# Turning the mixed channels for their statistics: VectorE block transposes in place of TensorE transposes, in the last pass over the second image

## The chip, the cores and the metric

The kernel runs on one core of a Trainium2 chip. Its metric is the device time of one execution in microseconds (us), the median of several runs. Everything is computed in fp32.

## The reference, cut to what matters

Two layers work on `x` of shape (2, 56, 56, 384): two images of 3136 tokens with 384 channels. The first is a neighbourhood attention with an MLP behind it. The second, in which the change lies, is this:

```python
h = _layernorm(x, n1_g, n1_b)
p = h @ w_in + b_in                       # 384 -> 768 channels
local = depthwise_conv3x3(p, k_conv)
lr, rl = ema along W, both directions
tb, bt = ema along H, both directions
mixed = 0.25 * (lr + rl + tb + bt) + local
mixed = _layernorm(mixed, on_g, on_b)     # over the 768 channels of a token
x = x + (mixed @ w_out + b_out)           # 768 -> 384
h2 = _layernorm(x, n2_g, n2_b)
m = gelu(h2 @ w1 + b1) @ w2 + b2          # 384 -> 1536 -> 384
return x + m
```

The line that matters is the layer norm of `mixed`. It needs the mean and the variance of each token over its 768 channels.

## The kernel before, in words

The kernel has three parts: the attention (to about 710 us), a pass that runs the first layer's MLP and the second layer's `w_in` while VectorE computes the convolution and the scans beside it, and the last pass, which runs `w_out` and the second layer's MLP and writes the output.

The convolution and the scans work with channels on partitions, so the mixed channels lie in memory as `mix_d`, 6 blocks of 128 channels by 3136 tokens per image. The last pass walks over all 6272 tokens in 13 groups (`dgroups`): eleven of 4 tiles of 128 tokens, then one of 3 and one of 2. Image 1 begins in the middle of group 6, and this group is called `half_way`.

For each group `load_mix` loads `mx`, 128 partitions by 6 blocks by up to 512 tokens, again with channels on partitions, and the residual `x`. That layout is what `project_out` wants as the stationary operand of its matmul, but it isn't what the statistics want: `bn_stats` on VectorE reduces along the free dimension, so tokens have to be on partitions. Thus `measure` turns each tile of `mx` for this purpose alone. In it TensorE transposes 6 blocks of 128 x 128 into two PSUM tiles `xi` (from the pool `ps_t`, three buffers), and VectorE takes `bn_stats` of each half and `bn_aggr` of both. The normalization itself is folded into `w_out` and its rows; of the statistics only the reciprocal standard deviation (`rs`) is used later. It scales the result of `project_out` when VectorE evicts it from PSUM (line 1258).

The instructions of each engine are issued in the order of the program text. One iteration of the last pass for group g is:

- the hidden layer: twelve blocks m of 128 hidden channels, each of three fp32 matmuls (line 1035) followed by a GELU on ScalarE (line 1044). Beside it `measure_beside` measures group g+1, one tile every other block: at m = 3, 5, 7 and 9. At m = 10 `close` computes `rs`, an addition on VectorE (line 219) and a power on GpSimd (line 222);
- `project_out` of group g+1: for each tile 6 matmuls with `w_out` (line 1051), the eviction with `rs` by VectorE into `x3` (line 1258), and the statistics of `x3` for the next layer norm;
- the loads of group g+2;
- the output layer: for each tile 12 matmuls with `w2` (line 1051), an addition by VectorE (line 1432) and the store. Between its tiles lie ScalarE's normalization of `x3`, GpSimd's addition of a bias (line 987), and TensorE's transposes of the normalized `x3` (line 251).

Both `project_out` and the output layer write the PSUM tile `y` of the pool `ps_y`, which has two buffers. The SBUF pool `cp` has a tag `work` with two buffers, which the convolution and the scans use. They are finished before group 6 is loaded, because the loop calls `beside.until((1, NI - 1))` there.

Of the kernel before, what the change touches and what calls it, by code (L numbers as in the profile page):

```python
# [40 lines left out]
B, H, W, C = 2, 56, 56, 384  # L41
NH, KS, HD = 12, 7, 32
P = 128
NC = C // P
INNER, NI = 2 * C, 2 * C // P
# [128 lines left out]
def block_kernel(ctx: ExitStack, tc: tile.TileContext, ins: dict, out: bass.AP):  # L174
    nc = tc.nc
# [438 lines left out]
    def norm_of(x, n, small):  # L614
        norm = Norm(small)
        for k in range(n):
            norm.add(k, [x[:, k, :]])
        return norm
# [14 lines left out]
    for h in range(0, NT, 2):  # L633
        norm = Norm(sm)
# [51 lines left out]
    units, ws, to_project, ahead, taking = {}, {}, [], [], []  # L686
# [4 lines left out]
    for s in range(NU + 4):  # L691
        n, k, hg, i = s // UG, s % UG, s % NC, s // NC
# [100 lines left out]
    norm = norm_of(xs[0], groups[0][1], sm)  # L793
# [154 lines left out]
    def passes(xs, xn, w1, w2, between=lambda psum: None):  # L948
# [11 lines left out]
        half_way = next(g for g, (t, n) in enumerate(dgroups) if t + n * P > T1)  # L960
# [102 lines left out]
        def flat(t):  # L1063
            return t.rearrange("p a b -> p (a b)")

        def half(name, tag, bufs=2):
            return cp.tile([P, HALF, W], F32, name=name, tag=tag, bufs=bufs)
# [152 lines left out]
        def load_mix(g):  # L1220
            t0, n = dgroups[g]
            mx = io.tile([P, NI, MT], F32, name="mx")
            for b, at, here, n in images(t0, n * P):
                nc.sync.dma_start(
                    out=mx[:, :, here : here + n],
                    in_=mix_d[b][:, :, at : at + n].rearrange("m p t -> p m t"),
                )
            x = load_group(x2_d, dgroups[g], "xa")
            if g >= half_way:
                add_row(x, dgroups[g][1], "b_out")  # L1230
            return mx, x, Norm(sm)

        def measure(mx, norm, k):
            parts = []
            for h in range(2):
                ps = ps_t.tile([P, NC, P], F32, name="xi", tag="pt")
                for c in range(NC):
                    nc.tensor.transpose(  # L1238
                        ps[:, c, :], mx[:, h * NC + c, k * P : (k + 1) * P], ident
                    )  # L1240
                parts.append(ps.rearrange("p c q -> p (c q)"))
            norm.add(k, parts)

        def measure_beside(m, g, ahead):

            n = dgroups[g][1]
            if m % 2 == 1 and 0 < m // 2 <= n:
                measure(ahead[0], ahead[2], m // 2 - 1)
            if m == 10:
                ahead[2].close(n)  # L1250

        def project_out(g, mx, x, inner):
            n = dgroups[g][1]
            x3 = io.tile([P, NT, C], F32, name="xc")
            norm = Norm(sm)
            for k in range(n):
                ps = tokens([mx[:, c, :] for c in range(NI)], w_out, k)
                nc.vector.scalar_tensor_tensor(  # L1258
                    x3[:, k, :], ps, inner.rs[:, k : k + 1], x[:, k, :], ALU.mult, ALU.add
                )  # L1260
                norm.add(k, [x3[:, k, :]])
                beside.go(OUT_D)
            norm.close(n)
            return x3, norm
# [62 lines left out]
        for g, (t0, n) in enumerate(groups):  # L1327
            hid = []
            preparing = prepare_w_out() if g == 1 else iter(())
            if g == last:  # L1330
                beside.until((0, NI - 1))
                load_row(0, "b2_1")
                ahead = load_mix(0)
            for m in range(NHID):
# [27 lines left out]
                if g == last:  # L1362
                    measure_beside(m, 0, ahead)
# [14 lines left out]
            norm = Norm(sm)  # L1378
# [15 lines left out]
        g, x2, norm_w = waiting  # L1394
# [3 lines left out]
        x3, norm = project_out(0, *ahead)  # L1398
# [8 lines left out]
        ahead = load_mix(1)  # L1407
# [5 lines left out]
        for g, (t0, n) in enumerate(dgroups):  # L1413
            hid = []
            for m in range(NHID):
                hid.append(hidden(w1, m, hT, n, "L1_conv_b1"))
                if g < last:
                    measure_beside(m, g + 1, ahead)
                beside.go(MLP_D)
            res = x3  # L1420
            if g < last:
                x3, norm = project_out(g + 1, *ahead)
            if g + 2 <= last and g + 2 != half_way:
                ahead = load_mix(g + 2)
            for k in range(n):
                if k == n - 1 and g < last:
                    hT = channels(xn, dgroups[g + 1][1], "L1_conv_n2_g", "L1_conv_n2_b")
                ps = tokens(hid, w2, k)
                o = res[:, k, :]
                if k == 0 and g < last:  # L1430
                    norm.shift(dgroups[g + 1][1])
                nc.vector.tensor_tensor(o, ps, o, ALU.add)  # L1432
                nc.sync.dma_start(out=yout[t0 + k * P : t0 + (k + 1) * P, :], in_=o)
                if k == n - 3 and g < last:
                    xn = normalized(norm, x3, dgroups[g + 1][1])
                    add_row(x3, dgroups[g + 1][1], "b2_1")
                beside.go(ROW_D)
            if g + 2 == half_way:
                beside.until((1, NI - 1))
                ahead = load_mix(g + 2)  # L1440
        pctx.close()

    def raise_flag(psum):
        ps = psum.tile([P, C], F32, name="y")
        nc.tensor.matmul(ps[:1, :1], lhsT=bad, rhs=ones[:, :1], start=True, stop=True)
        nc.vector.tensor_scalar(flag, ps[:1, :1], 1.0, 0.0, ALU.min, ALU.add)

    passes(xs, xn, w1, w2, raise_flag)
    again = nc.values_load(flag[0:1, 0:1], min_val=0, max_val=1)
    with tc.If(again > 0):  # L1450
        attention_again()
        w1, w2, w_parts = weights(0)
        for part in w_parts:
            part()
        xs = {g: load_group(x1f, groups[g], "xa") for g in range(2)}
        with tc.tile_pool(name="small_again", bufs=1) as sm_again:
            norm = norm_of(xs[0], groups[0][1], sm_again)
            norm.close(groups[0][1])
            norm.shift(groups[0][1])
            xn = normalized(norm, xs[0], groups[0][1])  # L1460
        passes(xs, xn, w1, w2)
# [69 lines left out]
```

## Time and profile before

| what | value |
|---|---|
| time, median of 3 runs | 2735.04 us (2734.52 to 2737.29) |
| span of the profiled run | 2733.8 us |
| hidden layer of group 6, with the measuring of group 7 | 2237.5 to 2270.6, 33.1 us |
| `project_out` of group 7 | 2270.6 to 2286.1, 15.5 us |
| VectorE busy in these two stages | 5.46 us and 4.08 us |
| transposes `xi` from 2240 us on | 126, in 2247.0 to 2651.4 us |
| `bn_stats` on `xi` from 2240 us on | 42, 556 ns each |

In the profile a line names its engine (PE is TensorE's matmul, PEld its loading of weights, DVE VectorE, ACT ScalarE, POOL GpSimd), the line of the kernel, the operation, its output and input tiles with their shapes, and how often it ran. A matmul in fp32 shows as two records, and a transpose as one: line 1051 has 2352 records for `w2` where the program has 2 layers x 49 tiles x 12 matmuls = 1176. Matmuls are pipelined, so the length of a record is more than what it adds to the time; the distance from one start to the next is what it adds.

### The profile page before, as it was taken

The page shows a single profiled execution, that of the slowest core. Times are in us where ns is not written, and L with a number is a line of the kernel's source. Part 1 is how long each engine was busy: PE and PEld are TensorE (multiplying, and loading weights), DVE is VectorE, ACT ScalarE, POOL GpSimd, SP SyncE. Part 2 cuts the span into 40 slices and gives each one's busy share as a digit, 9 for nine tenths or more (in the row PEclk, how much of TensorE's full clock was granted, in tenths as well). Part 3 has the DMA queues.
Part 4 walks back from the last instruction along what each step waited for, and adds up shares of the span by engine and source line. Part 5 has one row for each costly group of instructions (what it writes and reads, how often), then busy time and mean ns, then how long its engine had stood idle before and what let it go on. Part 6 is the DMA issues. An engine that isn't in the chain of part 4 may idle for free. (4 is left out here: it accounts for less than half of the span.)

```text
span 2733.8 us, 36207 instructions
## 1 busy us (share of the span) xinstructions
PE 2686.1 (98%) x14975; PEld 1505.5 (55%) x14975; DVE 1663.0 (61%) x2449; ACT 907.5 (33%) x1455; POOL 239.1 (9%) x256
## 2 busy tenths in 40 slices
PE   8999999999899999999999999999999999999998
PEld 4566656665655555555545555455555555555565
DVE  3778767777421188688988889888798422221110
ACT  4555555554322332222344422311233211111111
POOL 0111111110211100000000000000000011110100
PEclk9999999999999999999999999999999999999999
DMA  6322444224411122232355444433454410011000
GB/s 206 131 93 92 155 165 150 76 74 154 155 35 38 63 88 103 86 129 101 120 184 195 180 151 154 163 128 114 147 200 158 151 47 25 28 44 35 29 12 16
DMA packets 131887, 298.91 MB, mean 109 GB/s; under 512 B 10646, under 2 KB 87552, under 8 KB 129408
## 3 DMA queue, kind: packets, MB, share of 16 engines
q1 hardware_dynamic: 131712, 296.50, 31.2%
q8 instruction: 119, 1.95, 0.3%
q14 instruction: 56, 0.46, 0.1%
HBM read 180.86 MB, written 115.61 MB: 108 GB/s over the span
## 5 line engine op out<-in xcount | busy, mean ns | idle before, releaser
L1035 PE MATMUL mm<-hT,w 128*128 128x512 f32 (+2 forms) x1872 | 778.7, 571 | 3.9 <-ACT hid L1044 3.8
L1051 PE MATMUL y<-w,hid 128*128 128x384 f32 x2352 | 764.8, 486 | 0.0
L1051 PEld LDWEIGHTS y<-w,hid 128*128 128x128 f32 x2352 | 445.0, 190 | 305.2 <-issue 0.5
L1035 PEld LDWEIGHTS mm<-hT,w 128*128 128x128 f32 x1872 | 352.5, 191 | 378.1 <-issue 343.1
L1044 ACT ACTIVATE hid<-mm,chan 128x512 f32<-128x512 f32 (+2 forms) x312 | 206.0, 661 | 744.8 <-PE mm L1035 744.7
L1129 DVE SCALAR_TENSOR_TENSOR loc<-pt,taps,loc 128x990 f32<-128x990 f32 (+9 forms) x336 | 377.0, 1122 | 8.3
L521 DVE TENSOR_TENSOR pts<-sc,bias 119x448 f32<-119x448 f32 (+3 forms) x336 | 220.8, 699 | 97.9 <-PE sc L508 97.0
L528 ACT ACTIVATE pts<-pts 119x448 f32<-119x448 f32 (+3 forms) x336 | 206.5, 641 | 194.6 <-DVE pts L521 194.4
L222 POOL TENSOR_TENSOR rs<-rs,mhalf 128x4 f32<-128x4 f32 (+4 forms) x67 | 87.3, 1303 | 1794.5 <-DVE rs L219 1788.0
L385 PE MATMUL ps<-hT,wqkv 128*128 128x448 f32 x504 | 211.5, 558 | 0.6 <-ACT hT L361 0.4
L1051 PE MATMUL y<-w_out,mx 128*128 128x384 f32 x588 | 193.7, 489 | 3.2 <-DVE xc L1258 3.2
L1035 PE MATMUL mm<-hT,w_in 128*128 128x512 f32 (+2 forms) x468 | 191.7, 568 | 0.6 <-ACT hT L254 0.6
L1381 DVE TENSOR_TENSOR xc<-y,xa 128x384 f32<-128x384 f32 x49 | 27.3, 557 | 252.1 <-PE y L1051 251.7
L1432 DVE TENSOR_TENSOR xc<-y,xc 128x384 f32<-128x384 f32 x49 | 27.2, 556 | 219.5 <-PE y L1051 169.2
L1051 PEld LDWEIGHTS y<-w_out,mx 128*128 128x128 f32 x588 | 112.5, 191 | 84.7 <-issue 6.8
L508 PEld LDWEIGHTS sc<-qT,kT 32*100 32x100 f32 (+3 forms) x3168 | 97.8, 171 | 91.3 <-DVE pts L521 17.7
L240 ACT ACTIVATE xn<-xc,sh,rs 128x384 f32<-128x384 f32 x98 | 64.7, 698 | 248.6 <-DVE sh L233 248.4
L1035 PEld LDWEIGHTS mm<-hT,w_in 128*128 128x128 f32 x468 | 88.8, 190 | 101.5 <-issue 91.6
L214 DVE BATCH_NORM_STATS2 st<-xi 128x6 f32<-128x384 f32 x98 | 50.3, 554 | 154.2 <-PE xi L1238 154.1
L508 PE MATMUL sc<-qT,kT 32*100 32x112 f32 (+3 forms) x3168 | 130.9, 279 | 8.6 <-DVE pts L521 7.8
L385 PEld LDWEIGHTS ps<-hT,wqkv 128*128 128x128 f32 x504 | 90.0, 191 | 79.5 <-issue 74.8
L254 ACT ACTIVATE hT<-tp,chan 128x512 f32<-128x512 f32 (+2 forms) x117 | 79.4, 750 | 152.5 <-PE tp L251 152.4
(88 smaller groups left out, 2421.5 us busy)
## 6 DMA issues: line engine op xcount, KB each, us to landing
bias<-in_bias_t SPq DMA_DIRECT2D x16, 1344.0 KB
loc<-loc_d SPq DMA_DIRECT2D x24, 784.0 KB
mixed<-mix_d SPq DMA_DIRECT2D x24, 784.0 KB
mix_d<-mixed SPq DMA_DIRECT2D x24, 784.0 KB
xa<-x_d SPq DMA_DIRECT2D x22, 768.0 KB
p_d<-mx SPq DMA_DIRECT2D x10, 1536.0 KB
mx<-mix_d SPq DMA_DIRECT2D x10, 1536.0 KB
pt<-p_d SPq DMA_DIRECT2D x18, 560.0 KB
```

Source lines behind the costliest of these rows:

```text
L214: nc.vector.bn_stats(st[:n, i, :], x)
L222: nc.gpsimd.tensor_tensor(rs, rs, mhalf[:n, :k], ALU.pow)
L240: nc.scalar.activation(out[:, k, :], x[:, k, :], AF.Identity, bias=self.sh[:n, k : k + 1], scale=self.rs[:n, k : k + 1],)
L254: nc.scalar.activation(dst[:, c, : len(xs) * n], tp, AF.Identity, bias=col(b, c), scale=col(g, c))
L385: nc.tensor.matmul(ps, lhsT=wqkv[:, c, m * P : (m + 1) * P], rhs=hT[:, c, half_of(n)], start=c == 0, stop=c == NC - 1,)
L508: nc.tensor.matmul(sc[i // 2][: w.keys, i % 2, c * TT : (c + 1) * TT], lhsT=kT[d, hg, w.keys_at + r * w.kc : w.keys_at + (r + w.rows) * w.kc],
L521: nc.vector.tensor_tensor(self.of(half), sc[half][:n, :, : self.m * TT].rearrange("p h (c q) -> p h c q", q=TT), self.w.bias[:n, 4 * self. ...
L528: nc.scalar.activation(self.of(half), self.of(half), AF.Exp)
L1035: nc.tensor.matmul(ps[:, : n * P], lhsT=w[:, c, m * P : (m + 1) * P], rhs=hT[:, c, : n * P], start=c == 0, stop=c == NC - 1,)
L1044: nc.scalar.activation(t[:, : n * P], ps[:, : n * P], AF.Gelu, bias=col(b1, m))
L1051: nc.tensor.matmul(ps, lhsT=t[:, k * P : (k + 1) * P], rhs=w[:, m, :], start=m == 0, stop=m == len(lhs) - 1,)
L1129: nc.vector.scalar_tensor_tensor(to, pt[:, lo + dy - self.top : hi + dy - self.top, xt : xt + n], self.tap(dy, dx), to, ALU.mult, ALU.add,)
```

## The change

For the groups after `half_way`, 7 to 12, which lie wholly in the second image, a new function `measure_by_vector` takes the place of `measure`. VectorE can transpose 32 x 32 blocks. The function walks over the 4 x 4 grid of blocks of a 128 x 128 tile and turns, with each instruction, one such block in all six channel blocks at once: 32 partitions by 6 x 32 elements. A block that comes from the quadrant of partitions that starts at i is written to the quadrant that starts at j, so that 16 instructions together give the transpose of the whole tile in an SBUF tile `turned`. On this the same `bn_stats` and `bn_aggr` follow. The change is for TensorE, which no longer turns these tiles. The measuring of tile k is issued at block m = 2k, where it was at m = 2k + 3.

```diff
+        def measure_by_vector(mx, norm, k):
+            t = flat(half("turned", "work"))[:, : NI * P]
+            for i in range(0, P, HD):
+                for j in range(0, P, HD):
+                    nc.vector.transpose(
+                        t[j : j + HD].rearrange("p (m c) -> p m c", m=NI)[:, :, i : i + HD],
+                        mx[i : i + HD, :, k * P + j : k * P + j + HD],
+                    )
+            norm.add(k, [t[:, h * C : (h + 1) * C] for h in range(2)])
+
         def measure_beside(m, g, ahead):
             n = dgroups[g][1]
-            if m % 2 == 1 and 0 < m // 2 <= n:
+            if g > half_way:
+                if m % 2 == 0 and m // 2 < n:
+                    measure_by_vector(ahead[0], ahead[2], m // 2)
+            elif m % 2 == 1 and 0 < m // 2 <= n:
                 measure(ahead[0], ahead[2], m // 2 - 1)
             if m == 10:
                 ahead[2].close(n)
```

## The prediction, made before the changed kernel ran

> **What bounds the kernel now.** I read the engine totals first, then the busy time by stage, then the last pass instruction by instruction.
>
> The engine totals of the page:
>
> ```profile
> PE 2686.1 (98%) x14975; PEld 1505.5 (55%) x14975; DVE 1663.0 (61%) x2449; ACT 907.5 (33%) x1455; POOL 239.1 (9%) x256
> ```
>
> The busy time of each engine in the stretch from group 7's measuring to the end (columns: stretch, its length, then PE, PEld, DVE, ACT, POOL busy with instruction counts, granted clock, DMA share, GB/s):
>
> ```profile
> 2237.40:2733.80 496.40, 488.58 (x1545) 276.65 (x1543) 85.53 (x170) 78.82 (x123) 43.91 (x23) 1.00 0.09 31
> ```
>
> TensorE is busy for all but 7.8 of 496.4 us, and those lie behind its last matmul; VectorE is busy for 85.5 us. So here TensorE's work is the time, and VectorE has room. TensorE's timeline over the hidden layer of group 6, in which group 7 is measured (start, length, what):
>
> ```profile
> 2237.52 10.03 PE L1035 MATMUL mm<-hT,w 128*128 128x512 f32 x23
> 2247.39 0.82 PE L1238 MATMUL xi<-ident,mx 128*128 128x128 f32 x6
> 2248.05 5.32 PE L1035 MATMUL mm<-hT,w 128*128 128x512 f32 x12
> 2253.20 0.82 PE L1238 MATMUL xi<-ident,mx 128*128 128x128 f32 x6
> ...
> 2265.47 5.32 PE L1035 MATMUL mm<-hT,w 128*128 128x512 f32 x12
> 2270.62 4.68 PE L1051 MATMUL y<-w_out,mx 128*128 128x384 f32 x14
> ```
>
> A length contains the pipeline's tail; starts give the price. Six transposes take 2248.05 - 2247.39 = 0.66 us, twelve records of 512 columns take 2253.20 - 2248.05 = 5.15 us (0.429 each, two records for one fp32 matmul). No line shows idle time. VectorE over the same stretch, with the idle time before each entry in brackets:
>
> ```profile
> 2237.29 0.56 DVE L1432 TENSOR_TENSOR xc<-y,xc 128x384 f32<-128x384 f32 x1 [8.49 <-PE y L1051]
> 2247.92 1.03 DVE L214 BATCH_NORM_STATS2 st<-xi 128x6 f32<-128x384 f32 x2 [10.07 <-PE xi L1238]
> 2248.98 0.21 DVE L215 BATCH_NORM_AGGREGATE mv<-st 128x2 f32<-128x12 f32 x1
> ...
> 2266.65 0.16 DVE L219 SCALAR_TENSOR_TENSOR rs<-mv,ones 128x4 f32<-128x4 f32 x1
> 2274.76 0.62 DVE L1258 SCALAR_TENSOR_TENSOR xc<-y,rs,xa 128x384 f32<-128x384 f32 x1 [7.95 <-PE y L1051]
> 2275.41 0.56 DVE L214 BATCH_NORM_STATS2 st<-xc 128x6 f32<-128x384 f32 x1
> ```
>
> Between 2237.85 and 2274.76 VectorE has nothing to do but measure. GpSimd's power for `rs` follows the close:
>
> ```profile
> 2266.96 1.02 POOL L222 TENSOR_TENSOR rs<-rs,mhalf 128x4 f32<-128x4 f32 x1 [49.67 <-DVE rs L219]
> ```
>
> The costliest VectorE groups hold two of its own transposes, in the attention, and one op whose source is read across its lines (busy, mean ns, idle before):
>
> ```profile
> L1202 DVE SCALAR_TENSOR_TENSOR mixed<-line,mixed 128x392 f32<-128x392 f32 x96 | 77.5, 864 | 0.3 <-DMA mixed<-mix_d 0.2
> ...
> L481 DVE STREAM_TRANSPOSE turned<-sums 128x352 f32<-128x352 f32 x56 | 30.3, 542 | 0.5 <-PE sums L550 0.5
> ...
> L492 DVE STREAM_TRANSPOSE rec_t<-wide 128x352 f32<-128x352 f32 x56 | 30.0, 536 | 2.5 <-POOL wide L488 2.5
> ```
>
> [...] The new loop changes the output quadrant at every transpose[...]. The trace before has no such case. It shows the free one, two `bn_stats` of 556 ns in 1.03 us, so 0.47 apart, and the dependent one, 0.03 us after the end of the one before (2248.95 to 2248.98). I take the second. [...] The new patterns run 32 words at a time, on both sides. [...] L1202, whose source hops at every element, takes 864 ns for 392. [...] GpSimd's only work in this stretch is the 1.02 us of `rs`, which waits for VectorE anyway.
>
> **The change part by part.**
>
> *Removed from TensorE.* Groups 7 to 10 have 4 tiles, group 11 has 3, group 12 has 2: 21 tiles, 6 transposes each, 126. At 0.66, 0.65, 0.65 and 0.66 us per tile in the four gaps of this stage (mean 0.655) that is 21 x 0.655 = 13.76 us, all of it on an engine that never waits here. Group 6 (image border) keeps its transposes and its wait for the mixed channels.
>
> *Added to VectorE.* 16 transposes per tile, each 32 partitions x 192 elements. Price of one: VectorE's smallest ops of this form take 160 ns (the `rs` row, 0.16 us), so a transpose costs 160 + 1.07 per element ((536 - 160) / 352), and 192 elements cost 160 + 205 = 365 ns. That is an estimate. Its lower end is plain scaling, 536 x 192 / 352 = 292; its upper end is the whole 536, as if shortness saved nothing. I take 365 and 0.03 for the hold: 0.395 from start to start. The statistics of a tile stay: 1.03 + 0.03 + 0.21 + 0.04 = 1.31 us; that they now read SBUF is worth nothing I can see. One tile: 16 x 0.395 + 1.31 = 7.63 us. Four tiles: 30.5 us, against 36 matmuls x 0.858 = 30.9 us of TensorE work in the hidden layer.
>
> *Does VectorE finish in time?* In program order its next work behind the measuring is the eviction of `project_out`'s first tile (L1258), which also needs `rs`. It starts at 2237.88, with the mixed channels landed (in the view of transfers no such load is in flight from 2200 to 2240, and each later one lands some 50 us ahead of its use). It ends at 2268.4. From L219's start to the power's end is 2267.98 - 2266.65 = 1.33 us, so with 0.04 for handing over `rs` is there at 2269.8. The first tile of `project_out` used to be ready at 2274.76 and now is 2.62 us earlier, at 2272.14. So VectorE is 2.3 us ahead. And there is a second bank: `ps_y` has two buffers, so TensorE stalls only if the first isn't free when the third tile begins, at 2268.0 + 2 x 3.87 = 2275.74; the eviction must start by about 2275.0. Counted back, (2275.0 - 1.37 - 2237.88 - 4 x 1.31) / 64 = 0.476: up to this distance between transposes nothing is lost. Group 11's measuring has 3 tiles beside a hidden layer of 30.9 us, group 12's 2 tiles beside 72 x 0.322 = 23.2 us: both have room.
>
> *Moved.* Measuring begins at block 0, not 3, and `turned` takes the `work` buffers of the convolution, whose last user is finished before group 6 is loaded: no wait. `xi`'s PSUM buffers are used less. ScalarE, GpSimd and the transfers keep their orders; nothing of VectorE in the hidden layer is awaited by ScalarE. Cost nothing, hidden by TensorE's 30.9 us.
>
> Sum: 2735.04 - 13.76 = 2721.3 us.
>
> **The rivals.**
>
> *Part given back.* The distance is between 0.476 and 0.530, because a hold costs more than a dependence (0.08 more than my figure suffices). Each 0.01 above 0.476 stalls TensorE 0.64 us in each of the four full groups. At 0.50: 4 x 64 x 0.024 = 6.1 us, time 2727.5; at 0.530 all is given back. For it: the margin is only a fifth, and no held instruction is in the trace. Against: a dependent instruction already waits for the end of the one before, at 0.03.
>
> *VectorE becomes the bound, slower.* A transpose costs about 536 + 30 = 0.566, because its cost isn't in its length, or quadrant changes or the strided walk slow it. Four tiles then take 64 x 0.566 + 5.2 = 41.5 us, the eviction could start at 2280.7, 5.7 us too late, four times: 2735.04 - 13.76 + 22.8 = 2744.1. For it: 16 short instructions replace 6, the fixed part is 160 of 365 ns, and cross-quadrant writes are untried. Against: the smallest ops take 160 ns, so length does count.
>
> *Nothing moves.* TensorE waits for something else once the transposes are gone, a transfer or a GELU: 2735. Against it: no idle line on TensorE, ScalarE busy for 7.6 us of the 33 us, DMA share 0.09.
>
> **How the numbers follow.** Full gain 0.77, part given back 0.11, VectorE the bound 0.08, nothing moves 0.04. The predicted time is the first. About two thirds of the second case is still over 0.2% (5.5 us) faster, most of the rest within; so faster 0.84, same 0.07, slower 0.09. Range: the full gain with the spread of the times before (2734.52 to 2737.29, so -0.5 and +2.3) gives 2720 to 2724; the lower price of a transpose gives no more, as TensorE only loses 126 instructions; upwards I take the part of the second case to a distance of 0.50: 2719 to 2728.
>
> **What would show it.** On TensorE the hidden layers of groups 6 to 11 should be unbroken runs of 72 records and the period of a full group 2.6 us shorter; VectorE should be busy through nearly the whole hidden layer, with transposes of 0.36 to 0.38 us some 0.40 apart, the first eviction still released by TensorE's `y`. TensorE idle in `project_out`, released by VectorE or by `rs`, would show the second or third case. A distance over 0.476 proves the forecast wrong.

## The result, and the profile after

The changed kernel takes 2722.28 us (median of five runs, 2716.78 to 2726.42), the kernel before 2736.11 (2734.52 to 2737.45): ratio 0.9948, 95% interval 0.9933 to 0.9963. The forecast was 2721.3. A second measurement, on another occasion, gave 2721.68 against 2733.50, ratio 0.9959 (0.9946 to 0.9973).

The engine totals and the stretch from the start of group 6's hidden layer to the end (columns as before: PE, PEld, DVE, ACT, POOL busy with counts, clock, DMA share, GB/s):

```profile
PE 2666.7 (98%) x14849; PEld 1489.8 (55%) x14849; DVE 1786.4 (66%) x2785; ACT 907.2 (33%) x1455; POOL 238.8 (9%) x256
```

```profile
2235.75:2718.70 482.95, 475.08 (x1420) 264.05 (x1418) 207.06 (x506) 78.82 (x123) 43.90 (x23) 1.00 0.10 32
```

TensorE has 126 instructions fewer (14,849 for 14,975), VectorE 336 more, and in this stretch VectorE went from 85.5 to 207.1 us of busy time without TensorE noticing: its time without work is 482.95 - 475.08 = 7.9 us, as before, and lies behind its last matmul. TensorE's timeline of the changed kernel in one group:

```profile
2235.75 31.06 PE L1035 MATMUL mm<-hT,w 128*128 128x512 f32 x72
2266.65 15.64 PE L1051 MATMUL y<-w_out,mx 128*128 128x384 f32 x48
2282.13 23.38 PE L1051 MATMUL y<-w,hid 128*128 128x384 f32 x72
...
2314.40 31.06 PE L1035 MATMUL mm<-hT,w 128*128 128x512 f32 x72
```

The hidden layer is one unbroken run of 72 records, from start to start 30.90 us. The next group's begins at 2314.40, so the period of a full group is 78.65 us. In the kernel before, the same two starts are 81.28 us apart:

```profile
2237.09 10.46 PE L1035 MATMUL mm<-hT,w 128*128 128x512 f32 x24
...
2318.37 10.46 PE L1035 MATMUL mm<-hT,w 128*128 128x512 f32 x24
```

That is 2.63 us less, the price of four tiles' transposes (4 x 0.655 = 2.62). VectorE over the same hidden layer in the changed kernel (line numbers behind 1243 have moved by 15: 1273 is the old 1258, 1447 the old 1432):

```profile
2235.95 0.56 DVE L1447 TENSOR_TENSOR xc<-y,xc 128x384 f32<-128x384 f32 x1 [8.49 <-PE y L1051]
2236.42 6.11 DVE L1249 STREAM_TRANSPOSE turned<-mx 32x192 f32<-32x192 f32 x16
2242.56 1.02 DVE L214 BATCH_NORM_STATS2 st<-turned 128x6 f32<-128x384 f32 x2
2243.62 0.21 DVE L215 BATCH_NORM_AGGREGATE mv<-st 128x2 f32<-128x12 f32 x1
2243.74 6.06 DVE L1249 STREAM_TRANSPOSE turned<-mx 32x192 f32<-32x192 f32 x16
...
2265.69 0.16 DVE L219 SCALAR_TENSOR_TENSOR rs<-mv,ones 128x4 f32<-128x4 f32 x1
2270.79 0.62 DVE L1273 SCALAR_TENSOR_TENSOR xc<-y,rs,xa 128x384 f32<-128x384 f32 x1 [4.93 <-PE y L1051]
```

Sixteen transposes take 6.06 us, a tile 2243.74 to 2251.02 = 7.28 us, and no bracket shows VectorE waiting between them. The last line is the verdict: the first eviction is still released by TensorE's `y`, after 4.93 us in which VectorE had nothing to do. Its measuring is late for nobody.

To compare kernels more finely than whole runs allow, I use two pieces of the trace: A from the start of group 5's hidden layer to the end, which includes group 6's measuring, and B from the start of group 6's hidden layer. All kernels here do the same work ahead of A, and yet A began anywhere from 2144.9 to 2151.6 us in their profiles, so part of the spread of the medians has nothing to do with the edits. Some of it may be the clock: in these 13 profiles it was at half for 27 to 44 us ahead of A, and mostly longer where A began later (correlation 0.71). Each piece comes from one profiled execution. Five profiles are the same program from B's start on (the changed kernel twice, and the three of group 6), and their B lies between 482.86 and 482.99. A can contain a slow clock behind group 6's wait, as shown under that group: 1.5 of the 15.24 us by which the changed kernel's A is shorter come from there, and the other 13.76 are B's.

| kernel | median us | ratio to before (95%) | A | B |
|---|---|---|---|---|
| before | 2736.11 | 1 | 583.14 | 496.71 |
| changed | 2722.28 | 0.9948 (0.9933 to 0.9963) | 567.90 | 482.95 |
| changed, measured again | 2721.68 | 0.9959 (0.9946 to 0.9973) | 567.79 | 482.86 |
| no turning | 2720.82 | 0.9950 (0.9933 to 0.9966) | 569.36 | 482.94 |
| both engines turn | 2735.26 | 1.0001 (0.9992 to 1.0010) | 581.79 | 496.77 |
| 20 transposes a tile | 2718.81 | 0.9949 (0.9932 to 0.9965) | 568.86 | 483.70 |
| 24 transposes a tile | 2757.03 | 1.0082 (1.0065 to 1.0099) | 607.74 | 520.02 |
| orders of quadrants (one run) | 2717.53 | | 570.78 | 483.11 |
| group 6 split | 2718.10 | 0.9946 (0.9932 to 0.9959) | 567.64 | 482.99 |
| group 6 late on TensorE | 2714.47 | 0.9930 (0.9916 to 0.9944) | 564.47 | 482.96 |
| group 6 on VectorE | 2722.54 | 0.9961 (0.9946 to 0.9977) | 570.82 | 482.98 |
| MLP input on VectorE | 2711.64 | 0.9926 (0.9912 to 0.9939) | 559.77 | 476.06 |
| that, and group 6 late | 2706.02 | 0.9904 (0.9888 to 0.9919) | 556.40 | 476.20 |

### The profile page after: what moved, and what is told of

Its sections match the earlier page's. It is cut to its first block, busy times and chain, and to the rows that moved or that the text cites. A ratio compares the mean times of both kernels' runs of the same rounds, so it can differ in the third digit from the quotient of the medians.

```text
span 2718.7 us, 36291 instructions
## 1 busy us (share of the span) xinstructions
PE 2666.7 (98%) x14849; PEld 1489.8 (55%) x14849; DVE 1786.4 (66%) x2785; ACT 907.2 (33%) x1455; POOL 238.8 (9%) x256
## 5 line engine op out<-in xcount | busy, mean ns | idle before, releaser
L544 PE MATMUL o<-pts,vt 100*32 100x112 f32 (+3 forms) x3168 | 114.9, 269 | 12.0 <-DMA vt<-v_d 12.0
```

The source lines that it names most:

```text
L544: nc.tensor.matmul(o[i * HD : (i + 1) * HD, hg, :], lhsT=w.vt[:n, c, h * HD : (h + 1) * HD], rhs=self.pts[:n, i, c, :], start=c == 0, stop ...
```

## The experiments

### Is VectorE's work really free? No turning at all

```diff
-            t = flat(half("turned", "work"))[:, : NI * P]
-            for i in range(0, P, HD):
...
-            norm.add(k, [t[:, h * C : (h + 1) * C] for h in range(2)])
+            norm.add(k, [mx[:, h, : 2 * P] for h in range(2)])
```

> Groups 7 to 12 are not turned by any engine: the statistics are taken of mx as it lies, so the transposes are left out and the result is not the reference's. Theory (VectorE's transposes are wholly hidden behind TensorE's hidden layer): the same time as the changed kernel, 2722 us (2719 to 2725), last piece of the trace from the start of group 6's hidden layer 483.0 us as in the changed kernel. Rival (the transposes cost TensorE something that is hidden in the sum, by contention for memory or late evictions): 2 us or more below the changed kernel in that piece.

Piece B is 482.94 us, with the transposes 482.95. The 123 us that VectorE spends on them cost nothing: neither by late evictions nor by contention.

### Is the gain TensorE's own time? Both engines turn

```diff
             norm.add(k, [t[:, h * C : (h + 1) * C] for h in range(2)])
+            for h in range(2):
+                ps = ps_t.tile([P, NC, P], F32, name="xi", tag="pt")
+                for c in range(NC):
+                    nc.tensor.transpose(
+                        ps[:, c, :], mx[:, h * NC + c, k * P : (k + 1) * P], ident
+                    )
```

> VectorE turns and measures as in the changed kernel, and TensorE's six transposes per tile are issued as well, right behind, into PSUM tiles that nobody reads. Theory (the gain is TensorE's own time for 126 transposes, 0.655 us per tile): the gain is gone, 2722.3 + 13.8 = 2736 us, the last piece 496.7 us instead of 483.0. Rival (the gain came from a wait that VectorE's reading of PSUM or the release of the xi buffers caused): it stays at 2722 to 2728.

The gain is gone: ratio 1.0001, and B is 496.77, 0.06 from the kernel before. Nobody reads these `xi`, so it was not a wait for VectorE's reading that went, but 0.655 us of TensorE per tile. These transposes stand at the changed kernel's blocks, 2k, so the new place of the measuring isn't the gain either.

### How much more would VectorE have room for? 20 and 24 transposes

```diff
-            for i in range(0, P, HD):
-                for j in range(0, P, HD):
+            at = [(i, j) for i in range(0, P, HD) for j in range(0, P, HD)]
+            for i, j in at + at[:4]:
```

The second kernel has `at[:8]`.

> Four of a tile's 16 block transposes are issued a second time, 20 in all, each 0.38 us from start to start as the changed kernel's trace has it. A tile then takes 7.28 + 4 x 0.38 = 8.80 us, four 35.2, rs is there at 2236.4 + 35.2 + 1.4 = 2273.0 on the changed kernel's clock. The first tile of project_out is ready at 2270.8, the third wants its buffer at 2274.4. Theory (the second buffer of y absorbs a late eviction): no loss, 2722 (2720 to 2725). Rival (every microsecond behind the first tile's readiness is lost): 2.2 us in each of four groups, 2731.

> Eight of a tile's 16 block transposes are issued a second time, 24 in all. A tile takes 7.28 + 8 x 0.38 = 10.3 us, four 41.3, rs is there at 2279.1 on the changed kernel's clock, and the eviction should have started by 2273.7. Theory (VectorE becomes the bound just past the limit): 5.4 us lost in each of the four full groups, 2722.3 + 21.5 = 2744 us, TensorE idle in project_out until the eviction. Rival without the second buffer: 8.3 us four times, 2755. Rival (VectorE's work is hidden elsewhere too): 2722 to 2727.

With 20, `rs` arrives after the first tile of `project_out` is ready, and B grows by 0.75 us in all, not by 8.8; the periods of the full groups grow by 0.11 to 0.19. So the second buffer of `y` absorbs a late eviction, and 80 transposes per group are about the limit: what is lost per group is less than the 0.39 us of one of them. VectorE's timeline with 20 shows that `rs`, not `y`, now releases the eviction:

```profile
2268.61 0.16 DVE L219 SCALAR_TENSOR_TENSOR rs<-mv,ones 128x4 f32<-128x4 f32 x1
2269.97 0.62 DVE L1274 SCALAR_TENSOR_TENSOR xc<-y,rs,xa 128x384 f32<-128x384 f32 x1 [1.20 <-POOL rs L222]
```

With 24, TensorE stops behind the second tile, as the theory has it, but the loss is 37.1 us of B, not 21.5. The median, 2757.03, is nearest to the rival without the second buffer (2755), but that one would have TensorE stop behind the first tile, and the timeline shows that it doesn't:

```profile
2265.78 7.90 PE L1051 MATMUL y<-w_out,mx 128*128 128x384 f32 x24
2280.21 10.97 PE L1051 MATMUL y<-w_out,mx 128*128 128x384 f32 x24 [6.52 <-DVE xc L1274]
2291.01 23.38 PE L1051 MATMUL y<-w,hid 128*128 128x384 f32 x72
```

Two tiles (24 records, 24 x 0.3225 = 7.74 us) end at 2273.52, and the third starts 6.69 us later. The expectation was 5.4. Most of the difference comes from the repetition: a tile's 24 transposes take 9.40 us and not 9.1, so each of the eight that are issued again adds (9.40 - 6.06) / 8 = 0.42 us to the 16 of the changed kernel, and not 0.38. Why a repeated one costs more was not shown. But the tiles behind the gap take 2291.01 - 2280.21 = 10.80 us where two tiles took 7.74. The stretches of that time name the cause, in the column behind the counts, the granted clock:

```profile
2273.50:2280.20 6.70, 0.18 (x1) 0.00 (x0) 5.12 (x15) 0.00 (x0) 1.02 (x1) 0.68 0.00 0
2280.20:2284.00 3.80, 3.79 (x6) 2.19 (x7) 1.98 (x5) 0.00 (x0) 0.00 (x0) 0.50 0.00 0
2284.00:2288.00 4.00, 4.00 (x10) 2.20 (x9) 0.63 (x2) 0.00 (x0) 0.00 (x0) 0.72 0.00 0
```

After the wait TensorE runs at half its clock (0.50 from 2280.20 to 2284.00). The wait and the loss behind it, 6.69 + 3.06 = 9.75 us, are what this group's period grew by (88.40 for 78.65); the other three grew by 8.3 to 9.6. Taking the clock as either full (1.00) or half (0.50), the values of the second line and of the stretch behind the last (1.00 from 2288.00 to 2291.00), the three lines have it at half for 2 x 0.32 x 6.70 + 3.80 + 2 x 0.28 x 4.00 = 10.3 us. In the 6.0 us of these that lie in the last two lines the half clock cost half of the time, 3.0, and 3.06 were measured. The other 4.3 lie in the wait, so the clock fell about 2.4 us after the wait had begun. In the other three groups the clock was 0.71, 0.85 and 0.92 during the wait, and the loss behind it 1.51, 2.42 and 2.88 us: among these three the loss was the smaller, the more of the half clock fell into the wait itself.

### What makes a transpose 0.38 us? The order of quadrants

```diff
+            for s in range(16 if k == 0 else 8):
+                a, b = divmod(s, 4)
+                i, j = [(a, b), (0, 0), (b, 0), (0, b)][k]
...
+                nc.vector.transpose(to, mx[i : i + HD, :, k * P + j : k * P + j + HD])
```

> The transposes of groups 7 to 12 are measured by themselves; turned is not used and the statistics are taken of mx as it lies, so the result is not the reference's. Tile 0 of a group: the 16 transposes of the changed kernel. Tile 1: eight, all from quadrant 0 to quadrant 0. Tile 2: eight, the input's quadrant changing each time, the output in quadrant 0. Tile 3: eight, the input in quadrant 0, the output's quadrant changing each time. All 32 x 192. Theory (a change of quadrant holds an instruction until the one before has finished): tile 1 at 0.29 to 0.31 us from start to start, as the two bn_stats of 556 ns are 0.47 apart; tiles 0, 2 and 3 at 0.38. Rival (a transpose never overlaps with the next one): 0.38 in all four. Second rival (only the output's quadrant matters): tile 2 at 0.30 too.

VectorE's timeline has the four tiles one under the other:

```profile
2233.26 6.10 DVE L1255 STREAM_TRANSPOSE turned<-mx 32x192 f32<-32x192 f32 x16
...
2240.29 2.13 DVE L1255 STREAM_TRANSPOSE turned<-mx 32x192 f32<-32x192 f32 x8
...
2243.22 2.97 DVE L1255 STREAM_TRANSPOSE turned<-mx 32x192 f32<-32x192 f32 x8
...
2247.12 2.99 DVE L1255 STREAM_TRANSPOSE turned<-mx 32x192 f32<-32x192 f32 x8
```

Take off one transpose (0.37 us by its median, 0.32 in the second tile) and divide by the rest: 5.73 / 15 = 0.38, 1.81 / 7 = 0.26, 2.60 / 7 = 0.37, 2.62 / 7 = 0.37. Within one quadrant transposes overlap and come every 0.26 us; when the input's or the output's quadrant changes they don't. This is what the prediction calls a hold: a transpose that starts only when the one before has ended. There it was an estimate, as the trace before had no case of it; here it shows on both sides, and it costs about 0.12 us per transpose.

### Group 6: what the wait ahead of the changed part is worth

In the changed kernel TensorE still waits 3.47 us for `mx` of group 6, at its first transpose:

```profile
2164.74 0.84 PE L1238 MATMUL xi<-ident,mx 128*128 128x128 f32 x6 [3.47 <-DMA mx<-mix_d]
2165.42 5.32 PE L1035 MATMUL mm<-hT,w 128*128 128x512 f32 x12
```

In the kernel before, the same wait was followed by a slow clock (0.50 from 2164.30 to 2167.50). Six transposes from start to start took 1.31 us, and the twelve matmul records behind them 6.01:

```profile
2164.59 1.51 PE L1238 MATMUL xi<-ident,mx 128*128 128x128 f32 x6 [3.47 <-DMA mx<-mix_d]
2165.90 6.18 PE L1035 MATMUL mm<-hT,w 128*128 128x512 f32 x12
2171.91 0.82 PE L1238 MATMUL xi<-ident,mx 128*128 128x128 f32 x6
```

Three kernels treat this group otherwise.

Split, with tiles 0 and 1 on VectorE:

```diff
+            if g == half_way and m in (0, 2):
+                measure_by_vector(ahead[0], ahead[2], m // 2)
+            elif g == half_way:
+                if m in (7, 9):
+                    measure(ahead[0], ahead[2], m // 2 - 1)
```

> Group 6 on the image border, which TensorE still turns in the changed kernel and where TensorE stands 3.47 us until mx has landed: its tiles 0 and 1 are turned by VectorE, its tiles 2 and 3 by TensorE at blocks 7 and 9. Theory: VectorE waits for mx in TensorE's place (it is free then), TensorE's first transposes come at about 2171 us, after the landing at 2164.5; gain 3.47 + 2 x 0.655 = 4.8 us against the changed kernel, 2717.5 us. Rival (the wait moves to the eviction of project_out, which needs the residual's transfer behind mx): no gain, 2722.

Piece A is only 0.3 us shorter. The median, 2718.10, is where the theory had put it (2717.5), but by luck: the ratio to the kernel before, 0.9946, is no better than the changed kernel's 0.9948. The wait for `mx` has left TensorE, but not to the eviction, which the rival had named. TensorE's timeline shows where it went:

```profile
2173.56 0.49 PE L1238 MATMUL xi<-ident,mx 128*128 128x128 f32 x3
2176.82 0.60 PE L1238 MATMUL xi<-ident,mx 128*128 128x128 f32 x3 [2.77 <-DVE st L214]
2177.22 7.00 PE L1035 MATMUL mm<-hT,w 128*128 128x512 f32 x12
```

Two tiles need four `xi`, the pool has three, and VectorE, which had to start late, is still turning tile 1 when it should read the first of them. TensorE's restart is 2176.82 - 2173.56 - 3 x 0.109 = 2.93 us late, and its next twelve matmul records take 6.84 us instead of 5.15, at a granted clock of 0.56 from 2176.80 to 2180.00. Together that is 4.6 us, nearly all of the expected 4.8. So the clock fell with a wait of 2.93 us, too. Both theories of this run were wrong.

All on TensorE, but later:

```diff
+            if g == half_way:
+                if m in (7, 8, 9):
+                    for k in {7: [0], 8: [1], 9: [2, 3]}[m]:
+                        measure(ahead[0], ahead[2], k)
```

> Group 6 is turned by TensorE alone as in the changed kernel, but at blocks 7, 8 and 9 (two tiles at 9), after mx has landed. Theory: only the wait of 3.47 us goes, 2718.8 us. Rival: the wait returns at the eviction, because statistics and rs are then close to project_out: 2722.

A is 564.47, 3.43 us less than the changed kernel's, as expected. The median, 2714.47, moved further than that. One part may be the clock: the same wait of 3.5 us was followed by a slow stretch in four of the nine profiles that have it (those four are the kernel before, no turning, 24 transposes and orders of quadrants), at a loss of 1.4 to 2.8 us, and in five not. The longest of the nine waits, 3.68 us with 20 transposes, is one of the five. What that adds to a median isn't settled.

All on VectorE (`g >= half_way` in place of `g > half_way`):

> Group 6 is turned by VectorE alone. It can start when mx has landed, 13.7 us into the hidden layer: 2164.5 + 4 x 7.28 + 1.4 = 2195.0 us, where the eviction should start by 2188.7. TensorE saves the wait of 3.47 us and 4 x 0.655 = 2.6, and loses 6.3. Theory: the same within 1 us as the changed kernel, 2722.6, with an idle time of TensorE in project_out of group 6. Rival (a late start costs nothing): 6.1 us less, 2716.

The median is as expected, again by luck, for A is 2.92 us longer than the changed kernel's. TensorE's timeline:

```profile
2180.68 7.90 PE L1051 MATMUL y<-w_out,mx 128*128 128x384 f32 x24
2195.55 9.96 PE L1051 MATMUL y<-w_out,mx 128*128 128x384 f32 x24 [6.97 <-DVE xc L1273]
2205.35 23.38 PE L1051 MATMUL y<-w,hid 128*128 128x384 f32 x72
```

It restarts its third tile 7.13 us late (6.3 expected), and the next two tiles take 9.80 us where two take 7.74: 2.06 us more, at a clock of 0.55 in the first 4.5 of them, a cost that wasn't in the sum. An engine with room for the work still has to have the data in time.

### The same step elsewhere: the MLP's input

What the runs so far show is that a transpose taken from TensorE is worth its full 0.109 us if VectorE is idle then. The normalized `x3` is turned as well, three blocks per tile, in the output layer, where VectorE idles 7.2 us per tile. The changed kernel was measured again beside the two kernels that do this.

> The changed kernel as it is, beside the two that follow, so that they can be compared on one chip: 2722 us (2718 to 2726), last piece from the start of group 6's hidden layer 483.0 us.

```diff
+        def channels_by_vector(xn, n):
+            hT = io.tile([P, NC, MT], F32, name="hT")
+            for i in range(0, P, HD):
+                for j in range(0, P, HD):
+                    nc.vector.transpose(
+                        hT[j : j + HD, :, : n * P].rearrange("p c (k t) -> p k c t", k=n)[
+                            :, :, :, i : i + HD
+                        ],
+                        xn[i : i + HD, :n, :].rearrange("p k (c q) -> p k c q", c=NC)[
+                            :, :, :, j : j + HD
+                        ],
+                    )
+            return hT
...
                     add_row(x3, dgroups[g + 1][1], "b2_1")
+                    if g >= half_way - 1:
+                        hT_v = channels_by_vector(xn, dgroups[g + 1][1])
```

> The changed kernel, and the MLP's input of groups 6 to 12 (the normalized x3) is turned by VectorE too: 16 instructions of 32 x 384 per group into hT, then gain and bias by ScalarE in place. TensorE loses another 25 tiles x 3 transposes at 1.31 / 12 = 0.109 us, 8.2 us. VectorE needs about 16 x (0.160 + 384 x 1.07 ns) = 9.1 us between the second and the third tile of the output layer, where it has 7.2 us of idle time per tile and y has a second buffer; ScalarE's three passes end some 3 us before the next hidden layer. Theory (any of TensorE's turning that fits into VectorE's idle time is worth its full price): 8.2 us less than the changed kernel, 2714 us. Rival (the hidden layer waits for hT, or an eviction comes late): 2720 or more, with idle time of TensorE at the start of the hidden layer.

> The last kernel with, in addition, the late transposes of group 6 (blocks 7, 8 and 9). Theory: the two gains add, 8.2 and 3.4 to 6.2 (the wait, without and with the slow clock behind it): 2708 to 2711 us. Rival (they overlap): 2714.

A falls by 8.02 us with the input on VectorE (8.2 expected) and by 11.39 with group 6 late as well (8.2 + 3.4): the gains add. VectorE and then ScalarE in the combined kernel:

```profile
2289.53 9.31 DVE L1035 STREAM_TRANSPOSE hT<-xn 32x384 f32<-32x384 f32 x16
2298.87 0.56 DVE L1472 TENSOR_TENSOR xc<-y,xc 128x384 f32<-128x384 f32 x1
```

```profile
2298.87 2.23 ACT L1048 ACTIVATE hT<-hT,chan 128x512 f32<-128x512 f32 x3 [16.58 <-DVE hT L1035]
```

`hT` is ready at 2301.1, 3.2 us ahead of the hidden layer at 2304.34. The third tile's eviction waits for the transposes, and the second buffer hides that. This kernel takes 2706.02 us, against 2721.68 for the changed one beside it; the medians differ by more (15.7) than the piece does (11.4), and what makes the rest was not separated from the spread ahead of A.

## Why the prediction was right, point by point

- **What is removed.** 21 tiles at 0.655 us, 13.76 us. Piece B fell from 496.71 to 482.95, 13.76. A full group's period fell from 81.28 to 78.65. That it is TensorE's own time is shown by turning on both engines, where all of it returned.
- **The price of a transpose.** Estimated 0.365 us; measured 0.370 (median). From start to start I had 0.395, since I charged a hold like a dependence, 0.03, by estimate; it was 0.38, so a held transpose starts about 0.01 us after the end of the one before. Four tiles took 29.1 us, not 30.5.
- **The total.** That the median came within 1 us of the forecast is in part luck, as single runs of the changed kernel spread over almost 10 us. B is what shows that the sum was right.
- **In time or not.** `rs` should have been 2.3 us ahead of `y`. L219 at 2265.69 and 1.37 us behind it make 2267.06, 3.7 us ahead of the eviction at 2270.79.
- **The limit.** A distance of 0.476 was worked out as the last that costs nothing. The kernel with 20 transposes has 80 in a full group at 0.387, as much as 64 at 0.484, and lost 0.11 to 0.19 us per group: the limit is where it was put, and the second buffer is what sets it.
- **The rivals.** "VectorE the bound" would have come out worse than its 2744: my sum for it had only TensorE's wait, and the clock behind a wait of 6.7 us took another 1.5 to 3.1. The form was right, this term was missing. "Nothing moves" is refuted by B.
- **One reading was off.** I gave 2237.52 as the start of group 6's hidden layer; the view was cut there, and the start is 2237.09, so the layer took 33.5 us and not 33.1 (the table ahead of the prediction has the same reading). The working counted from the layer's end and didn't need it.

## What to carry to other kernels

Where one engine is busy without a gap, what its neighbour can take over is worth its start-to-start price, and the neighbour's price (here 6.1 us for 0.66) doesn't matter up to a limit that can be worked out beforehand: the next instruction in its queue that the first engine needs, plus the slack that a second buffer gives. Past the limit the loss was more than the wait here (9.75 us with a wait of 6.69), because TensorE's clock fell to half with it; and work that starts late because its data does is past the limit sooner.

## What was not expected of the hardware

- TensorE's clock after a wait: half of full speed (0.50 for 1.00), with a loss of 1.5 to 3.1 us behind each of five waits of 6.7 to 7.1 us, on top of the wait. With waits of about 3.5 us it fell in four of nine profiles, and with the one of 2.93 us too.
- The quadrant of partitions decides the pace of VectorE's short instructions: 32 x 192 transposes come every 0.26 us within one quadrant and every 0.37 to 0.38 when input or output changes quadrants. A cross-quadrant write as such adds nothing to be seen: in the changed kernel's trace the transposes that stay in their quadrant (i = j) and those that leave it both take 0.37 us.
